# A two-layer graph network on one core: clearing behind the gathers taken out, narrower sums, and 48 tiles fetched row by row by SyncE

## The chip, the cores and the metric

The kernel runs on one core of one Trainium2 chip. The metric is the device time of one execution in microseconds. TensorE (PE) multiplies matrices, VectorE (DVE) and ScalarE (ACT) work on tiles and copy out of the accumulators, GpSimd (POOL) issues the indirect gathers, and SyncE (SP) and ScalarE issue the other transfers.

## The reference

The graph has 12500 nodes with 128 features, 200000 edges sorted by their destination, and 8 relations. Two layers are run, then a residual and a layer norm. Cut to what matters:

```python
W = jnp.einsum('rb,bio->rio', comp, basis)
xw = jnp.einsum('ni,rio->nro', x, W)
msgs = xw[src, et]
seg = dst * N_REL + et
summed = segment_sum(msgs, seg)          # N_NODES * N_REL segments
cnt = segment_sum(ones, seg)
mean = summed / maximum(cnt, 1.0)[:, None]
h_new = relu(mean.reshape(N_NODES, N_REL, HIDDEN).sum(1) + x @ root + bias)
h = h_new + h                            # two layers of this
out = layernorm(x + h)
```

## The kernel before

**Tiles and octets.** The edges are cut into 1563 tiles of 128 in the order of their destinations; eight tiles are an octet (`Q = 8`, 196 octets, numbered `o` in layer 1 and `q` in layer 2). A tile of source rows is fetched by one indirect gather on POOL, a row of 512 bytes for each of the 128 edges.

**Layer 1.** For octet `o`, `gathers` puts the eight gathers of octet `o + 5` on POOL (`AHEAD = 5`, into one of seven `rows` buffers), `means` multiplies the eight row tiles by one-hot matrices that DVE makes, `product` multiplies by the weights, `place` and `finish` add up the nodes. `table` multiplies the finished nodes by layer 2's eight weight matrices and stores the result in DRAM as `y_d`, one row for each node and relation. In the octets from 96 to about 160 DVE, PE and SP also sort the edges of the routed octets (below): SP stores `lo_d` and `sc_d`, two small transfers for each.

**Layer 2** has two ways for an octet. In an ordinary octet POOL gathers rows of `y_d`, eight gathers, and `slot_sums` and `place_sums` add them up. A routed octet (`ROUTED`: octet 7 and every third after it, 62 in all) gets its sums from the node features that already lie on the chip: `compare` makes one-hot matrices on DVE, `pick_rows` picks the rows on PE (L1885), `slots_in` makes matrices of slots on DVE (L1852), `add_up` adds the picked rows into slots (L1905), and `relate` multiplies by the eight relations' weights (L1927). A slot is a node of the octet with a relation. The octet's eight tiles are taken as two parts of four (`BT = 4`), each with `NW = 40` nodes, so that `SEG = 8 * 40 = 320` slots go to each of two accumulators and `relate` gives 80 rows. Edges that found no place are fetched by one gather more (`gather_left`, L778). The steps of a routed octet are spread over the three octets ahead of it. So three octets in a row hold two ordinary ones and a routed one: 17 gathers on POOL, and one routing on PE and DVE.

**The clearing.** Behind each of layer 2's gathers POOL clears 256 bytes in each partition of a tile `blank` that nothing reads (`pause`, L712), and ahead of that it waits for the clearing before.

**Order.** The class `Plan` records every operation in program order with what it reads and writes, and derives the semaphore waits; nothing is reordered. Each engine runs its own operations in that order. Gathers have four semaphores in turn, SP's transfers eight. A gather into a `rows` buffer waits for the PE operation that read it last, so that POOL can run ahead of PE by the buffers it has. For the last six octets (`LATE = 6`) a gather also waits for PE's sums of the octet before (`after`). SP brings the node features (`load_x`), stores the sorted lists, and in layer 2 fetches for each routed octet a list of 256 KB and a small one (`fetch`, `fetch_rows`), when DVE has done with the buffer.

Of the kernel before, what the change touches and what calls it, by code (L numbers as in the profile page):

```python
# [9 lines left out]
F16 = mybir.dt.float16  # L10
I32 = mybir.dt.int32
BF16 = mybir.dt.bfloat16
AF = mybir.ActivationFunctionType
# [416 lines left out]
def ordered_path(  # L430
# [61 lines left out]
    FULL = NQ - 4  # L492
    BT = 4
    CAP = 32
    NW = 40
    BU = P // CAP
# [6 lines left out]
    GU = TU * BU  # L503
    SEG = R * NW
    BR = 2
    EVERY = 3
# [4 lines left out]
    NR = len(ROUTED)  # L511
    SORT = 96
    assert D == P and R * K == P and B == BF + 1 and 1 < TL and LAST < P and BF % 4 == 0 and Q == G and N % 2 == 0
    assert ROUTED[-1] < NQ - 4 and LATER % TURN == 0 and SORT + NR + 8 < NG - 16
# [99 lines left out]
    zero_b = part_of(P, "zero")  # L614
    which_b = [part_of(2 * NW, "which", i) for i in range(2)]
    kept_from = free_at
# [54 lines left out]

    plan = Plan(tc, {"hw": 8, "aq": 4, "gq": 4})
    plan.seen, plan.last = {}, {}
# [31 lines left out]
    rows_g = {}  # L705
    blank = keep([P, P // 2], F32, "blank").bitcast(mybir.dt.uint8)
    paused, pauses = tc.alloc_semaphore("s_pause"), [0]

    def pause():
        if pauses[0]:  # L710
            nc.gpsimd.wait_ge(paused, pauses[0])
        nc.gpsimd.memset(blank[:, :256], 0).then_inc(paused, 1)  # L712
        pauses[0] += 1


    def floats(t, n):
# [4 lines left out]
    fix_rows_c, fix_dm_c = ["jmp"], ["mixer"]  # L721
    y_done = [("y_d", j) for j in range(NT - 2)] + [("y_d", j, k) for j in (NT - 2, NT - 1) for k in (0, 1)]

    def gather(l, q):
# [19 lines left out]
        def some(i0, i1):  # L744
            def emit():
                ins = []
                if fixes:
                    ins.append(nc.gpsimd.indirect_dma_start(
                        out=fix_rows, out_offset=None, in_=y_d,
                        in_offset=bass.IndirectOffsetOnAxis(ap=fix_i[:, 0:1], axis=0)))  # L750
                for i in range(i0, i1):
                    ins.append(nc.gpsimd.indirect_dma_start(  # L752
                        out=t[:, i - q * Q, :], out_offset=None, in_=table_t,
                        in_offset=bass.IndirectOffsetOnAxis(ap=ids[:, i:i + 1], axis=0)))
                    if l == 1:
                        pause()
                return ins

            return emit
# [3 lines left out]
        if q == NQ - 2:  # L763
            for h in range(2):
                plan.add("POOL", some(i0 + h * 4, i0 + h * 4 + 4), reads, [cell + (h,)], lane="gq", n=4, after=after)
        elif l == 1 and q == NQ - 1:
            for i in range(n):
                plan.add("POOL", some(i0 + i, i0 + i + 1), reads, [cell + (i,)], lane="gq", n=1, after=after)
        else:
            plan.add("POOL", some(i0, i0 + n), reads,  # L770
                     [cell + (0,), cell + (1,)] + (fix_rows_c if fixes else []), lane="gq",
                     n=n + fixes, after=after)

    def gather_left(i):
        t, c = left_rows_b[i % len(left_rows_b)]

        def emit():
            ins = nc.gpsimd.indirect_dma_start(out=t, out_offset=None, in_=y_d,  # L778
                                               in_offset=bass.IndirectOffsetOnAxis(ap=idl[:, i:i + 1], axis=0))
            pause()  # L780
            return [ins]

        plan.add("POOL", emit, [idl_b[1]] + y_done, new(c), lane="gq", n=1)
# [402 lines left out]
    def onehot(l, q, g=None):  # L1186
# [11 lines left out]
        if l == 1 and q in ROUTED:  # L1198
            i = ROUTED.index(q)
            o, c = pl[q] = pl2_r.take()  # L1200
            vec(lambda: nc.vector.tensor_scalar(o[:2 * NW], cols[:2 * NW], pos2[:2 * NW, i:i + 1], None,
                                                op0=ALU.is_equal), ["cols", "pos2"], new(c))
# [101 lines left out]
    def means(o, half=None):  # L1304
# [4 lines left out]
        def some(i0, i1):  # L1309
            def emit():  # L1310
                for i in range(i0, i1):
                    last = nc.tensor.matmul(s_b[i // 4][0][:, i % 4, :], t[:, i, :],  # L1312
                                            d[:, i, :], start=True, stop=True)
                return last
# [5 lines left out]
        else:  # L1320
            pe(some(0, n), [c + (0,), c + (1,)] + dc,
               [s_b[h][1] for h in range(-(-n // 4))] + [("done", 0)])
# [170 lines left out]
    def values():  # L1493
# [10 lines left out]
        vec(lambda: nc.vector.memset(zero_at[0:1], 1.0), [], [zero_b[1]])  # L1504
        for b in range(2):
            vec(lambda b=b: nc.vector.memset(which_b[b][0][0:1, b * NW:(b + 1) * NW], 1.0), [], [which_b[b][1]])
        yield
# [28 lines left out]
        yield vec(lambda: nc.vector.tensor_scalar(i2, i1, float(NW), None, op0=ALU.mult), [ta_b[1]], [tb_b[1]])  # L1536
        vec(lambda: nc.vector.tensor_scalar(tb[:, :, BT:], tb[:, :, BT:], float(SEG), None, op0=ALU.add), [], [tb_b[1]])
        n4 = of_routed(near).rearrange("p n (b k) -> p n b k", k=BT)
        f0 = pt[:, 0, :2 * NR].rearrange("p (n b) -> p n b", b=2)
        pe(lambda: nc.tensor.matmul(f0, zero_at, n4[:, :, :, 0], start=True, stop=True), [zero_b[1]] + nears, [pc])  # L1540
        for b in range(2):
            pe(lambda b=b: nc.tensor.matmul(pt[:2 * NW, 1, :NR], which_b[b][0], n4[:, :, b, 0], start=b == 0,
                                            stop=b == 1), [which_b[b][1]] + nears, [pc])
        local = ta.rearrange("p n (b k) -> p n b k", k=BT)
        vec(lambda: nc.vector.tensor_tensor(local, n4, f0.unsqueeze(3).to_broadcast([P, NR, 2, BT]), op=ALU.subtract),
            nears + [pc], [ta_b[1]])
        vec(lambda: nc.vector.tensor_scalar(at_n[:, 1:2], part_f, float(NW), float(-NW), op0=ALU.is_ge, op1=ALU.mult),
            ["part_f"], ["at_n"])
        vec(lambda: nc.vector.tensor_tensor(at_n[:, 0:1], part_f, at_n[:, 1:2], op=ALU.add), ["part_f"], ["at_n"])
        yield vec(lambda: nc.vector.tensor_scalar(pos2[:2 * NW], pt[:2 * NW, 1, :NR], at_n[:2 * NW, 0:1], None,  # L1550
                                                  op0=ALU.add), [pc, "at_n"], ["pos2", "spread"])
        vec(lambda: nc.vector.tensor_tensor(val[:, :, :, 1], ta, tb, op=ALU.add), [ta_b[1], tb_b[1]], [val_b[1]])
# [176 lines left out]
    slot_b += [home(("sT1", "idx", "idx")[i], 2 * SEG, "slot", 5 + i) for i in range(3)]  # L1729
    sum_b = [home(("yr0", "yr1")[i], R * BR * NW, "sum", i) for i in range(2)]  # L1730
    segs_b = home("yr1", SEG, "segs")
# [164 lines left out]
    def add_up(t):  # L1896
# [14 lines left out]
        if u == NU - 1:  # L1911
            t_s, sc = sum_b[i % 2]
            t4 = t_s.rearrange("p (r b n) -> p r b n", r=R, b=BR)
            for k, (b, bc) in enumerate(seg_b):
                copy(t4[:, :, k, :], b.rearrange("p t d -> p (t d)")[:, :SEG].rearrange("p (r n) -> p r n", r=R), [bc],
                     new(sc + (k,)) if (sc + (k,)) in old else [sc + (k,)])
                plan.mark("ACT")

    for i in range(2):
        for k in range(BR):  # L1920
            old[sum_b[i][1] + (k,)] = old[sum_b[i][1]]

    def relate(i):
        t_s, sc = sum_b[i % 2]
        t4 = t_s.rearrange("p (r b n) -> p r b n", r=R, b=BR)
        b, bc = misc
        pe(in_turn([lambda r=r: nc.tensor.matmul(  # L1927
            b[:BR * NW, 0, :], t4[:, r].rearrange("p b n -> p (b n)"), w_sb[:, 1, r, :], start=r == 0, stop=r == R - 1)
            for r in range(R)]), [sc + (k,) for k in range(BR)] + [("w", 1, r) for r in range(R)], [bc])
        plan.mark("PE")  # L1930
        o, c = ys[ROUTED[i]] = ys_r.take()
        copy(o[:BR * NW], b[:BR * NW, 0, :], [bc], [c])
        plan.mark("ACT")
# [52 lines left out]
    def slot_sums(q):  # L1986
# [5 lines left out]
        def emit():  # L1992
            for i in range(Q):
                last = nc.tensor.matmul(m0[i // 2 * 2 * K:(i // 2 + 1) * 2 * K, :], d[:, i, :], t[:, i, :],  # L1994
                                        start=i % 2 == 0, stop=i % 2 == 1)
            return last

        pe(emit, [c + (0,), c + (1,), dc], [bc, ("done", 1)])
        plan.mark("PE")
# [4 lines left out]
    def place_sums(q, k, opens, last):  # L2004
# [4 lines left out]
        reads = [c, oc]  # L2009
        m = 2 * NW if q in ROUTED else P  # L2010
        if root_in:
# [267 lines left out]
    for o in range(NG - 3):  # L2279
# [3 lines left out]
        means(o)  # L2283
        batch(o)
        if o == 1:
            where()
# [134 lines left out]
    for q in range(NQ):  # L2421
# [28 lines left out]
        if q == 0:  # L2450
            turn_last()
        if q == FROM - 1:
            compare(0)
# [105 lines left out]
```

## Time and profile before

| what | value |
|---|---|
| median of 3 runs | 3645.96 us (3643.89 to 3647.16) |
| the profiled execution | 3643.43 us, its span 3641.3 us |
| busy in the span | PE 2870.5 us, POOL 2942.4 us, DVE 2290.1 us, ACT 665.8 us |
| gathers of layer 1 | 1563, mean 957 ns |
| gathers of layer 2 | 1067, mean 953 ns, and 62 of `gather_left` |
| clearings | 1129, mean 329 ns |
| mean granted clock of TensorE | 0.893 of full speed |

In the profile a row of the groups gives the line of the code, the engine, the operation, the tiles written and read, the shape and the count, then the busy time in us and the mean of one in ns, and the time that the engine stood idle ahead of it with what ended most of that wait. "issue" is time in which an engine waited for nothing that the profile shows. Matmuls of 32-bit numbers stand twice in the records: a product of eight matrices reads x16. In the rows by windows each engine's busy time in the stretch is followed by the number of its instructions.

### The profile page before, as it was taken

Reading aid. Unit: us, or ns where it says so; the run is one execution under the profiler, and the core shown is the slowest. Engines: PE = TensorE matmul, PEld = TensorE weight load, DVE = VectorE, ACT = ScalarE, POOL = GpSimd, SP = SyncE. Lnnn points to the kernel's source line nnn. Section 1 sums busy time; section 2 is a strip of 40 time slices with the busy share of each in tenths; the row PEclk is TensorE's granted clock in tenths of the full one; section 3 lists DMA queues with packets and bytes.
Section 4 is the critical chain, followed back from the end, with each engine's and each line's share of the span. In section 5 each row is a group of like instructions: output and inputs, shape, how many; then the busy total and the mean of one; then the engine's idle time right before and its main releaser. Section 6 shows DMA issues by size and latency. Waiting matters only on the chain.

```text
span 3641.3 us, 68810 instructions
## 1 busy us (share of the span) xinstructions
PE 2870.5 (79%) x27639; PEld 2299.7 (63%) x27639; DVE 2290.1 (63%) x6306; ACT 665.8 (18%) x1725; POOL 2942.4 (81%) x3830
## 2 busy tenths in 40 slices
PE   6777667777677777777777499999989988998994
PEld 4665556666666666666665267767666666666663
DVE  5655444543478787873331378877777777786773
ACT  1121112222222222222222011111111111111110
POOL 7777777777777777777776888888888888888887
PEclk8998888888888888888889799999999999999997
DMA  4221233333222222223333322222222222222221
GB/s 132 59 54 53 53 88 99 92 99 99 82 77 82 76 76 77 76 73 99 94 99 106 86 59 59 71 70 65 65 67 71 59 70 67 59 71 67 65 59 55
DMA packets 134922, 275.89 MB, mean 76 GB/s; under 512 B 56995, under 2 KB 65741, under 8 KB 134597
## 3 DMA queue, kind: packets, MB, share of 16 engines
q0 software_dynamic: 86176, 176.66, 18.8%
q1 hardware_dynamic: 31450, 42.72, 3.9%
q10 hardware_dynamic: 16971, 52.05, 3.7%
q8 instruction: 219, 3.59, 0.4%
q14 instruction: 106, 0.87, 0.1%
HBM read 211.95 MB, written 59.28 MB: 74 GB/s over the span
## 4 chain that ended last, share of the span: by engine, by line
POOL 65%; issue 15%; PE 13%; DVE 3%; DMA 2%; ACT 1%; POOLq 0%; ACTq 0%; DVEq 0%
POOL rows L752 55%; POOL blank L712 8%; PE s L1312 2%; PE pt L1885 2%; PE y L1344 2%; PE y L1905 1%; POOL arena L778 1%; PE po L1905 1%; DVE dm L1219 1%; DMA rows<-in_x_dram,idx 1%; PE pt L1443 1%; PE ct L958 1%; DVE arena L948 1%; DMA rows<-y_d,idy 1%; PE s L2025 1%
## 5 line engine op out<-in xcount | busy, mean ns | idle before, releaser
L752 POOL DMA_INDIRECT rows<-in_x_dram,idx x1563 | 1496.0, 957 | 478.1 <-issue 471.1
L752 POOL DMA_INDIRECT rows<-y_d,idy x1067 | 1016.8, 953 | 195.2 <-issue 175.4
L1312 PE MATMUL s<-dm,rows 128*128 128x128 f32 x3126 | 544.8, 347 | 403.1 <-DMA rows<-in_x_dram,idx 383.8
L1312 PEld LDWEIGHTS s<-dm,rows 128*128 128x128 f32 x3126 | 509.0, 255 | 469.2 <-issue 319.1
L1219 DVE TENSOR_SCALAR dm<-cols,kr,w 128x128 f32<-128x128 f16 x1563 | 525.3, 401 | 226.2 <-PE ct L1443 133.9
L1344 PE MATMUL y<-w_sb,sT 128*128 128x128 f32 x3136 | 460.6, 310 | 45.8 <-ACT sT L692 45.6
L1344 PEld LDWEIGHTS y<-w_sb,sT 128*128 128x128 f32 x3136 | 446.4, 227 | 56.2 <-ACT sT L692 54.1
L1885 PE MATMUL pt<-arena,dm 128*32 128x128 f32 x12152 | 408.9, 283 | 5.1 <-DVE dm L1835 4.6
L1885 PEld LDWEIGHTS pt<-arena,dm 128*32 128x32 f32 x12152 | 337.9, 114 | 57.2 <-issue 39.9
L712 POOL MEMSET blank<- 128x256 uint8 x1129 | 371.0, 329 | 0.7
L692 ACT ACTIVATE sT<-s 128x512 f32<-128x512 f32 x391 | 212.2, 594 | 841.7 <-PE s L1312 841.7
L1905 PE MATMUL y<-arena,dm 128*128 128x320 f32 x620 | 242.0, 473 | 35.2 <-DVE arena L1852 34.8
L1178 DVE TENSOR_SCALAR sT<-cols,kr,w 128x32 f32<-128x32 f16 x1040 | 238.3, 302 | 19.3 <-PE s L2029 19.2
L1835 DVE TENSOR_TENSOR dm<-arena,cols 128x768 f32<-128x768 f16 x248 | 231.6, 934 | 5.4 <-DMA arena<-lo_d 3.3
L1905 PE MATMUL po<-arena,dm 128*128 128x320 f32 x620 | 219.1, 435 | 0.0
L1396 DVE TENSOR_TENSOR po<-po,carry 128x128 f32<-128x128 f32 x98 | 28.8, 294 | 299.9 <-PE ct L1443 146.0
L692 ACT ACTIVATE dm<-pt 128x256 f32<-128x256 f32 x248 | 95.0, 383 | 585.3 <-PE pt L1885 585.3
L1994 PE MATMUL ct<-rows,sT 128*32 128x128 f32 x2080 | 91.5, 291 | 115.0 <-DMA rows<-y_d,idy 115.0
L1905 PEld LDWEIGHTS y<-arena,dm 128*128 128x128 f32 x620 | 105.2, 194 | 93.8 <-DVE arena L1852 35.1
L1852 DVE TENSOR_SCALAR arena<-cols,comp_sb 128x640 f32<-128x640 f16 x155 | 140.3, 938 | 37.5 <-DMA arena<-y_d,arena 37.5
L692 ACT ACTIVATE y_row<-pt 128x512 f32<-128x512 f32 (+1 forms) x133 | 79.4, 597 | 413.8 <-PE ct L1443 182.8
L1994 PEld LDWEIGHTS ct<-rows,sT 128*32 128x32 f32 x2080 | 55.3, 113 | 157.1 <-DMA rows<-y_d,idy 75.9
(336 smaller groups left out, 3987.4 us busy)
## 6 DMA issues: line engine op xcount, KB each, us to landing
y_d<-y_row ACTq DMA_DIRECT2D x96, 512.0 KB
rows<-in_x_dram,idx POOLq DMA_INDIRECT x1563
rows<-y_d,idy POOLq DMA_INDIRECT x1067
arena<-lo_d SPq DMA_DIRECT2D x62, 256.0 KB
x_g<-in_x_dram SPq DMA_DIRECT2D x24, 512.0 KB
out_dram<-x_g SPq DMA_DIRECT2D x12, 512.0 KB
arena<-in_L_gnn_basis_dram SPq DMA_DIRECT2D x2, 512.0 KB
w_d<-y_row SPq DMA_DIRECT2D x2, 512.0 KB
```

The lines of the kernel that those rows point to most:

```text
L692: act(lambda: nc.scalar.activation(out_t, in_t, AF.Copy), reads, writes)
L712: nc.gpsimd.memset(blank[:, :256], 0).then_inc(paused, 1)
L752: ins.append(nc.gpsimd.indirect_dma_start(out=t[:, i - q * Q, :], out_offset=None, in_=table_t, in_offset=bass.IndirectOffsetOnAxis(ap=ids ...
L1178: vec(in_turn([lambda i=i: nc.vector.tensor_scalar(t[:, i, :], cols[:, :2 * K], kr[:, i0 + i:i0 + i + 1], w[:, i0 + i:i0 + i + 1], op0=ALU ...
L1219: emits.append(lambda i=i: nc.vector.tensor_scalar(t[:, i - q * Q, :wide], cols[:, :wide], ids[:, i:i + 1], w[:, i:i + 1], op0=ALU.is_equa ...
L1312: last = nc.tensor.matmul(s_b[i // 4][0][:, i % 4, :], t[:, i, :], d[:, i, :], start=True, stop=True)
L1344: last = nc.tensor.matmul(y[:m], t[:, r, :nt, :].rearrange("p t k -> p (t k)"), w_sb[:, 0, r, :], start=(r == 0), stop=(r == R - 1))
L1835: emits = [lambda: nc.vector.tensor_tensor(o[:, :3 * n].rearrange("p (j c) -> p j c", j=3), bits[:, None, u * n:(u + 1) * n].to_broadcast( ...
L1852: vec(lambda v=v, o=o: nc.vector.tensor_scalar(o, segs_p, sg[:, v:v + 1], sg[:, NTL + v:NTL + v + 1], op0=ALU.is_equal, op1=ALU.mult), ["n ...
L1885: last = nc.tensor.matmul(b[k * CAP:(k + 1) * CAP, x, :], o[:n, c:c + CAP], hT[:n, j * P:(j + 1) * P], start=jj == 0, stop=jj == SIZE[g] - 1)
L1905: last = nc.tensor.matmul(b.rearrange("p t d -> p (t d)")[:, :SEG], g[:, x * P:(x + 1) * P], o[:, k * SEG:(k + 1) * SEG], start=v == 0, st ...
L1994: last = nc.tensor.matmul(m0[i // 2 * 2 * K:(i // 2 + 1) * 2 * K, :], d[:, i, :], t[:, i, :], start=i % 2 == 0, stop=i % 2 == 1)
```

## The change

It has four parts. `pause` and its tile are gone. The routed octets' slots are numbered over one span of `NW = 76` nodes for all eight tiles, so that there are 608 slots, 304 to each accumulator, and `relate` gives 76 rows; the preparation in `values` is shorter for it. For 27 tiles of layer 1 (tile 183 and every 50th after it) and 21 of layer 2 (tile 95 and every 72nd) POOL issues no gather: SP issues 128 transfers of one row each into one of two buffers, in 8 chunks of 16, and each chunk first loads 16 addresses from DRAM into SP's registers. The scratch of GpSimd's transfers is 8192 in place of the default.

```diff
-    NW = 40
+    NW = 76
-    SEG = R * NW
-    BR = 2
+    SEG = R * NW // 2
+    RC = 16
+    SINGLES = [("SP", 0, range(183, NQ * Q - 80, 50)), ("SP", 1, range(95, (NQ - 4) * Q, 72))]
...
-    plan = Plan(tc, {"hw": 8, "aq": 4, "gq": 4})
+    plan = Plan(tc, {"hw": 8, "aq": 4, "gq": 4, "sr": 8, "ar": 8})
-    def pause():
-        if pauses[0]:
-            nc.gpsimd.wait_ge(paused, pauses[0])
-        nc.gpsimd.memset(blank[:, :256], 0).then_inc(paused, 1)
-        pauses[0] += 1
+    def single_rows(l, o):
+        for i, (e, at_l, ts) in enumerate(SINGLES):
+            if at_l != l:
+                continue
+            t8 = (x if l == 0 else y_d).bitcast(U8)
+            for k, t in enumerate(ts):
+                for c in range(P // RC):
+                    if (t - ts.step - 2 * Q + c * ts.step * RC // P) // Q != o:
+                        continue
+                    b = hw_b[e][k % 2].bitcast(U8)
+
+                    def emit(e=e, i=i, k=k, c=c, b=b):
+                        eng = by[e]
+                        eng.reg_load(regs[e], off_d[i][k:k + 1, c * RC:(c + 1) * RC])
+                        return [eng.dma_start(b[c * RC + j:c * RC + j + 1, :], bass.AP(
+                            tensor=t8.tensor, offset=eng.snap(r), ap=[[4 * D, 1], [1, 4 * D]]))
+                            for j, r in enumerate(regs[e])]
+
+                    plan.add(e, emit, [("off", i)] + (y_done if l else []), [("hw_" + e, k % 2, c)],
+                             lane="sr" if e == "SP" else "ar", n=RC)
...
                 for i in range(i0, i1):
+                    if (l, i) in SINGLE:
+                        continue
                     ins.append(nc.gpsimd.indirect_dma_start(
...
-                    if l == 1:
-                        pause()
...
-    nc = _bacc.Bacc("TRN2", target_bir_lowering=False, num_devices=1)
+    nc = _bacc.Bacc("TRN2", target_bir_lowering=False, num_devices=1, dynamic_dma_scratch_size=8192)
```

The program's order shows the parts at three places. On POOL, in layer 2, before: the end of one octet, the gather of a routed octet's left edges (`arena<-y_d,arena`) and the start of the next octet.

```order
L752 DMA rows_105<-y_d,idy 128x128
L712 MEMSET blank 128x256 [waits s_pause]
L778 DMA arena<-y_d,arena 128x128 [waits s_gq3,s_DVE]
L712 MEMSET blank 128x256 [waits s_pause]
L752 DMA rows_106<-y_d,idy 128x128 [waits s_PE]
L712 MEMSET blank 128x256 [waits s_pause]
L752 DMA rows_106<-y_d,idy 128x128
```

The same place after, where octet 11 has one of its eight tiles from SP and so only seven gathers.

```order
L800 DMA rows_105<-y_d,idy 128x128 [waits s_gq2,s_PE]
L800 DMA rows_105<-y_d,idy 128x128 x7
L824 DMA arena<-y_d,arena 128x128 [waits s_gq3,s_DVE]
L800 DMA rows_106<-y_d,idy 128x128 [waits s_PE]
L800 DMA rows_106<-y_d,idy 128x128 x6
```

Nothing stands between two gathers any more, and the waits for PE and DVE are at the places where they were.

On SP, in the sorting part of layer 1, before: the two stores of three octets.

```order
L689 DMA lo_d<-arena 32x32 [waits s_ACT]
L689 DMA sc_d<-arena 32x2x32 [waits s_ACT]
L689 DMA lo_d<-arena 32x32 [waits s_ACT]
L689 DMA sc_d<-arena 32x2x32 [waits s_ACT]
L689 DMA lo_d<-arena 32x32 [waits s_ACT]
L689 DMA sc_d<-arena 32x2x32 [waits s_hw3,s_ACT]
```

After, chunks of rows (`TENSOR_LOAD` is the load of 16 addresses, `x16` the 16 transfers) stand between the stores; the next rows of the order go on in the same way.

```order
L699 DMA lo_d<-arena 32x32 [waits s_ACT]
L699 DMA sc_d<-arena 32x2x32 [waits s_ACT]
L752 TENSOR_LOAD off_d_156 [waits s_sr0]
L753 DMA hw_SP_152<-in_x_dram 1x512 x16
L752 TENSOR_LOAD off_d_156 [waits s_sr1]
L753 DMA hw_SP_152<-in_x_dram 1x512 x16
L699 DMA lo_d<-arena 32x32 [waits s_ACT]
L699 DMA sc_d<-arena 32x2x32 [waits s_ACT]
```

A store now has up to 32 transfers ahead of it on SP, and the chunks wait in turn behind the stores, which wait for ACT. In layer 2 the fetches stand between the chunks in the same way.

On PE, in layer 2, after: the routed octet's sums and the octet whose eighth tile (`hw_SP_152`) SP has brought.

```order
L1941 MATMUL y<-arena,dm 128x304
L1941 MATMUL po_138<-arena,dm 128x304
L2029 MATMUL ct<-rows_106,sT_112 32x128 [waits s_sr4,s_sr3,s_sr5,s_sr2,s_sr6,s_sr1,s_sr7,s_sr0,s_gq0]
L2029 MATMUL ct<-rows_106,sT_112 32x128 x6
L2029 MATMUL ct<-hw_SP_152,sT_112 32x128
L2062 MATMUL s_135<-pl_116,ys_118 128x256
```

Before, the same place reads:

```order
L1905 MATMUL y<-arena,dm 128x320
L1905 MATMUL po_138<-arena,dm 128x320
L1994 MATMUL ct<-rows_106,sT_112 32x128 [waits s_gq0]
L1994 MATMUL ct<-rows_106,sT_112 32x128 x7
L2025 MATMUL s_135<-pl_116,ys_118 128x256
```

The order of PE's work is the same; the sums are 304 wide in place of 320, and the whole octet waits for the eight chunks of its row-by-row tile.

More of the change, by code (lines that the diff above doesn't have):

```diff
@@ L11 @@
 I32 = mybir.dt.int32
+U8 = mybir.dt.uint8
 BF16 = mybir.dt.bfloat16
@@ L512, in ordered_path @@
     SORT = 96
+    RC = 16
+    SINGLES = [("SP", 0, range(183, NQ * Q - 80, 50)), ("SP", 1, range(95, (NQ - 4) * Q, 72))]
+    SINGLE = {(l, t): (i, k) for i, (_, l, ts) in enumerate(SINGLES) for k, t in enumerate(ts)}
+    LISTED = (14, NQ - 24)
+    assert all(l == 0 or all(t // Q not in ROUTED and t // Q < NQ - 4 for t in ts) for _, l, ts in SINGLES)
+    assert len(SINGLE) == sum(len(ts) for _, _, ts in SINGLES)
     assert D == P and R * K == P and B == BF + 1 and 1 < TL and LAST < P and BF % 4 == 0 and Q == G and N % 2 == 0
@@ L670, in ordered_path @@
     nb_f = keep([1, 1], F32, "nb_f")
-    plan = Plan(tc, {"hw": 8, "aq": 4, "gq": 4})
+    hw_b = {e: [keep([P, D], F32, f"hw_{e}{i}") for i in range(2)] for e in {e: 0 for e, _, _ in SINGLES}}
+    offs = [keep([P, len(ts)], I32, f"off{i}") for i, (_, _, ts) in enumerate(SINGLES)]
+    off_d = [dram.tile([len(ts), P], I32, name=f"off_d{i}") for i, (_, _, ts) in enumerate(SINGLES)]
+    by = {"SP": nc.sync, "ACT": nc.scalar}
+    regs = {e: [by[e].alloc_register(f"row_{e}{i}") for i in range(RC)] for e in hw_b}
+    plan = Plan(tc, {"hw": 8, "aq": 4, "gq": 4, "sr": 8, "ar": 8})
     plan.seen, plan.last = {}, {}
@@ L722, in ordered_path, with single_lists, single, singles_in @@
     y_done = [("y_d", j) for j in range(NT - 2)] + [("y_d", j, k) for j in (NT - 2, NT - 1) for k in (0, 1)]
+    def single_lists(l):
+        for i, (_, at_l, ts) in enumerate(SINGLES):
+            if at_l != l:
+                continue
+            ids, name = (idx, "idx") if l == 0 else (idy, "idy")
+            n = len(ts)
+            blocks_i = range(ts.start // P, ts[-1] // P + 1)
+            picked = ids[:, ts.start:ts.start + n * ts.step].rearrange("p (n k) -> p n k", k=ts.step)[:, :, 0]
+            vec(lambda i=i, picked=picked: nc.vector.tensor_single_scalar(
+                offs[i], picked, 9, op=ALU.logical_shift_left),
+                [(name, b) for b in blocks_i], [("offs", i)])
+            plan.mark("DVE")
+            load(bass.AP(tensor=off_d[i].tensor, offset=off_d[i].offset, ap=[[1, P], [P, n], [1, 1]]),
+                 offs[i].unsqueeze(2), [("offs", i)], [("off", i)])
+    def single_rows(l, o):
+        for i, (e, at_l, ts) in enumerate(SINGLES):
+            if at_l != l:
+                continue
[13 more added lines that the diff above has]
+                             lane="sr" if e == "SP" else "ar", n=RC)
+    def single(l, t):
+        if (l, t) not in SINGLE:
+            return None
+        i, k = SINGLE[l, t]
+        e = SINGLES[i][0]
+        return hw_b[e][k % 2], [("hw_" + e, k % 2, c) for c in range(P // RC)]
+    def singles_in(l, i0, i1):
+        return [single(l, i) for i in range(i0, i1) if (l, i) in SINGLE]
     def gather(l, q):
@@ L1729, in ordered_path @@
     slot_b += [home(("sT1", "idx", "idx")[i], 2 * SEG, "slot", 5 + i) for i in range(3)]
[L1730 removed]
+    sum_b = [home(("yr0", "yr1")[i], 2 * SEG, "sum", i) for i in range(2)]
     segs_b = home("yr1", SEG, "segs")
@@ L1919, in ordered_path @@
     for i in range(2):
-        for k in range(BR):
+        for k in range(len(seg_b)):
             old[sum_b[i][1] + (k,)] = old[sum_b[i][1]]
```

60 lines of the change are left out of this document (26 added, 34 removed).

## The prediction

> **What bounds the kernel now.** I read the busy time in slices and the chain of waits first (the page), then POOL's groups, then single stages in the windows.
>
> ```profile
> PE   6777667777677777777777499999989988998994
> ...
> POOL 7777777777777777777776888888888888888887
> PEclk8998888888888888888889799999999999999997
> ...
> POOL 65%; issue 15%; PE 13%; DVE 3%; DMA 2%; ACT 1%; POOLq 0%; ACTq 0%; DVEq 0%
> POOL rows L752 55%; POOL blank L712 8%; PE s L1312 2%; PE pt L1885 2%; PE y L1344 2%; PE y L1905 1%; POOL arena L778 1%; PE po L1905 1%; DVE dm L1219 1%; DMA rows<-in_x_dram,idx 1%; PE pt L1443 1%; PE ct L958 1%; DVE arena L948 1%; DMA rows<-y_d,idy 1%; PE s L2025 1%
> ```
>
> 80% of the chain is POOL and the gaps between its instructions; 8% are the clearings. But PE is at 9 tenths in layer 2 (the last 17 slices), so PE stands close behind POOL there. POOL's groups and their pace by stage (the windows of L752, then of L712, columns: stretch, length, busy and count):
>
> ```profile
> L752 POOL DMA_INDIRECT rows<-in_x_dram,idx x1563 | 1496.0, 957 | 478.1 <-issue 471.1
> L752 POOL DMA_INDIRECT rows<-y_d,idy x1067 | 1016.8, 953 | 195.2 <-issue 175.4
> L712 POOL MEMSET blank<- 128x256 uint8 x1129 | 371.0, 329 | 0.7
> ```
>
> ```profile
> 30.00:690.00 660.00, 499.11 (x529) 0.87 0.25 71
> 1000.00:1600.00 600.00, 457.37 (x469) 0.83 0.27 77
> ...
> 2094.00:3540.00 1446.00, 328.98 (x1001) 0.97 0.25 66
> ```
>
> In layer 1 a gather takes 660/529 = 1.248 us from start to start (0.96 of work, 0.30 of gap), in the sorting stage 600/469 = 1.279. In layer 2 one comes every 1446/1001 = 1.445 us: 0.95 of gather, 0.165 of gap, 0.33 of clearing. "issue" ends 471 of the 478 us of idle time in the one layer and 175 of 195 in the other, so no gather waits long but at the end of layer 1, and both layers go at POOL's pace. How far PE is behind in layer 2 shows in the routed octets, one for every three octets (17 gathers). These rows are the first and the last `relate`, then all engines in two stretches, and the records of `relate` (16 a time) in the first of them:
>
> ```profile
> 2108.84 1.91 PE L1927 MATMUL po<-w_sb,y_row 128*80 128x128 f32 x16
> ...
> 3570.03 3.17 PE L1927 MATMUL po<-w_sb,y_row 128*80 128x128 f32 x14
> ```
>
> ```profile
> 2224.00:2419.00 195.00, 191.65 (x2615) 143.77 (x2614) 164.12 (x421) 33.25 (x98) 172.42 (x271) 1.00 0.26 71
> 2420.00:3540.00 1120.00, 1010.02 (x13267) 755.88 (x13268) 826.85 (x2080) 160.50 (x488) 990.91 (x1551) 0.96 0.25 65
> ```
>
> ```profile
> 2224.00:2419.00 195.00, 17.19 (x144) 16.45 (x145) 1.00 0.26 71
> ```
>
> Over the layer the 61 steps from one routed octet to the next take (3570.03 - 2108.84)/61 = 23.95 us. From 2224 to 2419 us PE is busy 98% at full clock, catching up after a late start: there it does 144/16 = 9 routed octets in 195 us, 21.67 us each. That is PE's own pace, and DVE is at 84% in it. So POOL can become faster by 2.3 us in 24 before PE takes over.
>
> **The clearing.** Its removal shortens a gather's period in layer 2 from 1.445 to about 1.248 us if the gap behind a gather is then 0.30 as in layer 1. Layer 2 has one gather with nothing behind it:
>
> ```profile
> 2019.89 1.22 POOL L748 DMA_INDIRECT jmp<-y_d,fix_i  x1 [1.11 <-DMA y_d<-y_row]
> 2021.42 0.94 POOL L752 DMA_INDIRECT rows<-y_d,idy  x1 [0.30 <-issue]
> ```
>
> The gap is 0.30 there. Below, the bound is 1.248, above it the sorting stage's 1.279, where DVE is at 80%. Three octets cost POOL 17 x 1.248 = 21.2 us, and with 21 gathers fewer over 65 triples 16.67 x 1.248 = 20.8 (21.3 at 1.279).
>
> **The narrower sums.** PE's products with 320 columns follow each other at 0.54 us at full clock:
>
> ```profile
> 2107.76 0.70 PE L1905 MATMUL y<-arena,dm 128*128 128x320 f32 x2
> 2108.30 0.70 PE L1905 MATMUL po<-arena,dm 128*128 128x320 f32 x2
> ```
>
> 304 columns make 0.513. A routed octet has 16 of them (eight tiles, two accumulators): 0.43 us less, 21.67 - 0.43 = 21.24. DVE's slots shrink in the same share, off the path. If the octets' spans were over 76 nodes, the kernel would take its general path; in the inputs the widest of the 62 has 69.
>
> So PE (21.24) and POOL (20.8 to 21.3) come out nearly equal, and PE is a little behind. I take 21.3 a step, PE's pace and little for the waits that two equal engines cause. The bounds: 20.8, if PE's 2% of idle time in that stretch also goes, and 21.67/0.96 = 22.6, if the narrower sums give nothing and the clock stays at the second stretch's 0.96. The forecast is 61 x (23.95 - 21.3) = 162 us, with ends of 192 and 82.
>
> **The start and the end of layer 2.** DVE and so PE wait for the first gather of left edges:
>
> ```profile
> DVE arena L1852 <- DMA arena<-y_d,arena: 37.5, 1, 37.5
> ...
> L778 POOL DMA_INDIRECT arena<-y_d,arena x62: 950/950/953, 2079.1 to 3577.0; - x62
> ```
>
> It has 56 ordinary gathers of layer 2 ahead of it on POOL (octets 0 to 6): 56 x 0.197 = 11 us earlier. At the end the gathers of the last octets wait for PE's sums, so that POOL's pace counts again: octets 191 to 194 and the three tiles of octet 195 are 35 gathers, 35 x 0.197 = 7 us.
>
> **The rows by SP.** In layer 1 they take 27 gathers off POOL, 10 of them in the sorting stage: 17 x 1.248 + 10 x 1.279 = 34 us, if SP keeps up. In layer 2 the 21 are already in the 20.8. The price of a row on SP isn't in the trace. The nearest issue is that of a single run, the others are SP's loads of one word and its register work:
>
> ```profile
> L689 SPq DMA_DIRECT2D arena<-in_edge_type_dram x1: 249/249/249, 11.6 to 11.6; - x1
> ...
> L689 SPq DMA_DIRECT2D sc_d<-arena x62: 368/423/762, 998.0 to 1624.9; - x62
> ```
>
> ```profile
> L2184 SPq TENSOR_LOAD <-bad x1: 498/498/498, 2828.1 to 2828.1; - x1
> L2184 SPq FUSED_REGOPS  x1: 192/192/192, 2828.7 to 2828.7; - x1
> L2184 SPq SEQ_ASSERT  x1: 28/28/28, 2828.9 to 2828.9; - x1
> ```
>
> ```profile
> 4.02 0.37 ACTq L689
> 4.40 0.04 issue
> ```
>
> A row is one register move and one issue. With 0.25 for the issue, 0.03 to 0.19 for the move and a gap of 0.04 behind each (the last fence, from the chain of the first 25 us, where ACT issues transfers one behind the other), it costs 0.36 to 0.52 us; I take 0.37, nearest to the small instruction, since a move is one step and not several fused. A chunk's load costs at least 0.50 + 0.04, so a tile costs SP 128 x 0.37 + 8 x 0.54 = 52 us (71 at 0.52). Layer 1 gives it 50 x 1.248 = 62 us and layer 2 nine octets, 3 x 21.3 = 64. In the sorting stage SP also issues two stores, 0.30 and 0.42 us, in each octet of 10.2 us: 1.28 chunks of 6.5 and 0.8 make 9.1 of 10.2. So SP is hidden behind POOL at 0.37, is filled in the sorting stage from 0.42 and everywhere from 0.45. Behind SP's rows stand `lo_d`, `sc_d` and layer 2's fetches, each delayed by a chunk or two (7 to 13 us); the buffers that they free or fill are wanted two octets (16 us) later or more. On PE the octet with such a tile waits for its eight chunks, and behind that wait stands the next routing; SP has the last chunk issued some 22 tiles (27 us) ahead. I cost both at nothing; when this lead is gone, the first rival begins.
>
> [...]
>
> **The scratch.** [...] A gather lands 2.5 us after its issue, so that two or three are under way:
>
> ```profile
> 283.90 2.48 DMA rows<-in_x_dram,idx
> ```
>
> [...]
>
> **The sum.** 34 + 11 + 162 + 7 = 214 us off the profiled execution's 3643.4: 3429. The median of the runs is 2.5 us above that execution, so 3432.
>
> **The rivals.** *SP becomes the bound* (slower). Layer 1's first chunk can go at octet 14, about 155 us; then come 27 tiles, about 80 us of rest of the layer and 20 of its end, 21 tiles, and 60 us to the end: 315 + 48 tiles' price. At 64 us a tile that begins to show; at 69.3, a row of 0.51 us, it is as slow as now, and at the upper bound's 71.4 it gives 3742. The 192 ns speak for it, the 249 and the 28 against. [...]
>
> *The clearing isn't what held the gathers* (the change doesn't do what it says): POOL stays at 1.445 in layer 2, be it by the scratch or by something that the clearing hides. Then only the fewer gathers count, 34 + 21 x 1.445 = 64 us: 3579, with the median's 2.5 some 3582. The gap of 0.30 behind L748 speaks against it.
>
> *PE loses more than it should*: it waits for late rows or left edges in every step and falls to half clock in between (granted 0.96 in the second stretch, 1.00 in the first). At the bound of 22.6 us a step, 61 x 1.3 = 79 us more: 3511.
>
> **How the numbers follow.** Forecast, between 3400 and 3470: 0.67. PE's longer steps, or SP somewhat over its period, 3470 to 3620: 0.19, half of it under 3510. The clearing without effect: 0.05. SP so slow that the kernel is slower than now: 0.07, the 0.02 in it. Below 3400: 0.02. The range is 3398 to 3515; it leaves out some 0.2 above. About 0.2% is what a measurement of this kernel can tell from no change. Faster 0.91, same 0.02, slower 0.07: only SP's row price between 0.505 and 0.51 us would give the same.
>
> **What would show it.** In the changed profile L752's successor has no clearing behind it and 1.25 us from start to start where PE lets it; POOL has waits for PE in layer 2, PE is at 97% or more there at a clock near 1.00, and `relate` comes every 21.3 us. Layer 1 ends 34 us earlier. SP's row issues stand at 0.37 us. Wrong would be: PE waiting for `hw_SP` in both layers (the first rival), gathers still 1.4 us apart with nothing between them (the second), or steps over 22 us with PE idle (the third).

## The result, and the profile after

The changed kernel takes 3798.57 us (median of 4 runs, 3793.73 to 3799.97) against 3644.93 us before (4 runs, 3643.50 to 3647.16), measured side by side: ratio 1.0419, 95% interval 1.0401 to 1.0437. It is slower by 4%; the forecast was 3432 us. The profiled execution took 3793.73 us with a span of 3791.9 us, at a granted clock of 0.862 (before 0.893).

From the page of the changed kernel: busy tenths in the slices of PE and POOL, the granted clock, and the chain of work that ended last, by engine and by line.

```profile
PE   6757455574555666566455558999899899899996
...
POOL 7777777577567566566666457777766766666653
PEclk8988788787787788788778789999999999999998
...
SPq 65%; issue 17%; PE 9%; DVE 3%; DMA 2%; POOL 1%; ACT 1%; ACTq 0%; POOLq 0%; DVEq 0%
SPq L753 39%; SPq L752 19%; SPq L754 5%; SPq L699 2%; PE y L1390 2%; POOL rows L800 1%; PE s L1358 1%; PE pt L1921 1%; DVE dm L1264 1%; PE y L1941 1%; PE pt L1489 1%; PE po L1941 1%; DVE arena L993 1%; DMA off_d<-off 0%; PE ct L1003 0%
```

Before, 80% of this chain were POOL and the gaps between its instructions. Now 65% are SP, and the lines are those of the single rows: the row transfers (L753), the loads of addresses (L752) and a register move (L754). POOL has fallen from 7 and 8 tenths to 5 to 7. SP's work is not in the busy table, since issuing a transfer does not count as busy there; the chain shows it nonetheless.

A stretch of the chain in the middle of layer 1 (start, length, line), with the end of one chunk of 16 rows, a whole chunk, and two loads:

```profile
591.36 0.23 SPq L753
591.74 0.23 SPq L753
592.13 0.23 SPq L753
592.52 0.23 SPq L753
592.75 0.05 issue
592.80 2.04 SPq L752
594.98 0.26 SPq L753
...
600.83 0.23 SPq L753
601.11 1.96 SPq L752
```

A row follows the row before it after 0.39 us, and between two chunks stands a load of some 2 us. SP's instructions over the whole program, grouped by line and tile (min/median/max in ns, first and last start), the fix-up gather that ends layer 1, and `relate`:

```profile
L752 SPq TENSOR_LOAD <-off_d x384: 1878/2004/6879, 195.4 to 3744.7; - x192
...
L753 SPq DMA_DIRECT2D hw_SP<-in_x_dram x3456: 13/228/733, 197.5 to 2115.4; - x192
...
L753 SPq DMA_DIRECT2D hw_SP<-y_d x2688: 227/228/299, 2244.4 to 3753.2; - x192
...
L754 SPq MOVE  x6144: 16/34/312, 197.4 to 3753.0; - x199
```

```profile
L794 POOL DMA_INDIRECT jmp<-y_d,fix_i x1: 1028/1028/1028, 2231.2 to 2231.2; - x1
```

```profile
L1961 PE MATMUL po<-w_sb,y_row x992: 272/273/273, 2312.3 to 3729.4; 128*76 128x128 f32 x199
```

In layer 1 a tile takes SP (2115.4 - 197.5)/27 = 71.0 us, in layer 2 (3753.2 - 2244.4)/21 = 71.8. Layer 1 was to give it 62.4 us a tile and layer 2 some 64. So layer 1 ends late: its fix-up gather starts at 2231.2 us in place of 2019.9, 211 us later. Layer 2 is shorter than before, but its routed octets come every (3729.4 - 2312.3)/61 = 23.2 us, not every 21.3.

Who waits, in the changed kernel (engine, line, what it waited for: us in total, times, longest):

```profile
PE s L1358 <- DMA hw_SP<-in_x_dram: 495.2, 26, 37.6
...
PE po L1899 <- DMA dm<-sc_d: 97.9, 26, 6.8
...
PE ct L2029 <- DMA hw_SP<-y_d: 23.1, 1, 23.1
```

```profile
POOL rows L800 <- PE s L1358: 252.1, 36, 42.3
...
ACT arena L702 <- DMA lo_d<-arena: 239.2, 53, 13.4
...
POOL rows L800 <- PE ct L2029: 183.6, 33, 52.7
...
DVE dm L1871 <- DMA arena<-lo_d: 153.3, 37, 7.5
```

In layer 1 PE waits 26 times for a row tile, once for each tile but one, and POOL then waits for PE to free the buffers. In the sorting stage ACT waits 239 us for SP's stores of `lo_d`, which stand behind rows too. In layer 2 PE hardly waits for the rows themselves (23 us). It waits for `sc_d`, and DVE for `lo_d`: the fetches that stand behind the rows on SP. All engines in most of layer 2:

```profile
2260.00:3660.00 1400.00, 1260.98 (x17080) 961.73 (x17081) 1050.41 (x2666) 206.97 (x627) 967.04 (x1025) 0.95 0.26 69
```

In this stretch (length, then busy time and count of PE, PEld, DVE, ACT and POOL, then the clock, DMA share and GB/s) PE is busy 90% at a clock of 0.95; without rows it comes to 98% at 1.00 (the next section).

Eight of the runs below were made while the kernel before itself took 4569 to 4666 us; nothing is concluded from their times, and for that reason all eight kernels were run again.

### The profile page after: what moved, and what is told of

Same layout as the page of the kernel before. It is cut to its first block, busy times and chain, and to the rows that moved or that the text cites. A ratio compares the mean times of both kernels' runs of the same rounds, so it can differ in the third digit from the quotient of the medians.

```text
span 3791.9 us, 86653 instructions
## 1 busy us (share of the span) xinstructions
PE 2711.9 (72%) x27635; PEld 2180.3 (57%) x27635; DVE 2273.5 (60%) x6303; ACT 659.7 (17%) x1725; POOL 2520.9 (66%) x2653
## 4 chain that ended last, share of the span: by engine, by line
SPq 65%; issue 17%; PE 9%; DVE 3%; DMA 2%; POOL 1%; ACT 1%; ACTq 0%; POOLq 0%; DVEq 0%
SPq L753 39%; SPq L752 19%; SPq L754 5%; SPq L699 2%; PE y L1390 2%; POOL rows L800 1%; PE s L1358 1%; PE pt L1921 1%; DVE dm L1264 1%; PE y L1941 1%; PE pt L1489 1%; PE po L1941 1%; DVE arena L993 1%; DMA off_d<-off 0%; PE ct L1003 0%
## 5 line engine op out<-in xcount | busy, mean ns | idle before, releaser
L800 POOL DMA_INDIRECT rows<-in_x_dram,idx x1536 | 1472.9, 959 | 711.7 <-issue 452.8
L800 POOL DMA_INDIRECT rows<-y_d,idy x1046 | 987.4, 944 | 511.2 <-issue 305.8
L1358 PE MATMUL s<-dm,rows 128*128 128x128 f32 x3072 | 423.8, 294 | 523.8 <-DMA hw_SP<-in_x_dram 495.2
L1358 PEld LDWEIGHTS s<-dm,rows 128*128 128x128 f32 x3072 | 402.9, 208 | 564.7 <-issue 534.8
L1941 PE MATMUL y<-arena,dm 128*128 128x304 f32 x620 | 237.2, 465 | 28.6 <-DVE arena L1888 28.6
L1941 PE MATMUL po<-arena,dm 128*128 128x304 f32 x620 | 213.6, 427 | 0.0
L1660 DVE TENSOR_TENSOR arena<-ct,arena 128x256 f32<-128x256 f32 x62 | 26.1, 421 | 216.8 <-PE y L1700 175.0
L1888 DVE TENSOR_SCALAR arena<-cols,comp_sb 128x608 f32<-128x608 f16 x155 | 135.3, 907 | 30.3 <-DMA arena<-y_d,arena 30.3
L1489 PE MATMUL pt<-w_sb,arena 128*128 128x512 f32 (+1 forms) x262 | 141.5, 623 | 9.6 <-ACT y_row L702 8.2
L1941 PEld LDWEIGHTS po<-arena,dm 128*128 128x128 f32 x620 | 121.3, 196 | 43.7 <-issue 4.4
```

Of the source, the lines that this page charges most:

```text
L800: ins.append(nc.gpsimd.indirect_dma_start(out=t[:, i - q * Q, :], out_offset=None, in_=table_t, in_offset=bass.IndirectOffsetOnAxis(ap=ids ...
L1941: last = nc.tensor.matmul(b.rearrange("p t d -> p (t d)")[:, :SEG], g[:, x * P:(x + 1) * P], o[:, k * SEG:(k + 1) * SEG], start=v == 0, st ...
```

## The experiments

Each version was measured side by side with the kernel before on the same chip. The versions were on several chips; on each the kernel before took 3643 to 3645 us. The eight runs set aside stand at the end of this section.

**Without the rows.**

```diff
-    SINGLES = [("SP", 0, range(183, NQ * Q - 80, 50)), ("SP", 1, range(95, (NQ - 4) * Q, 72))]
+    SINGLES = []
```

> [...] Theory A, SP's work on the rows is the whole loss: 3466 us (ratio to before 0.951). Theory B, one of the other three parts cost the time: 3640 us or above (ratio 1.00 or more).

Measured: 3449.48 us (3447.77 to 3452.07), ratio 0.9464 (0.9449 to 0.9480). Its chain, the window from 2094 to 3380 us (columns as above), POOL's gaps without another wait (us in total, times, longest), the end of layer 1 and `relate`:

```profile
PE 45%; POOL 37%; issue 12%; DVE 2%; DMA 2%; ACT 2%; POOLq 0%; ACTq 0%; DVEq 0%
```

```profile
2094.00:3380.00 1286.00, 1262.43 (x17553) 966.00 (x17547) 1070.91 (x2725) 212.76 (x647) 963.98 (x1021) 1.00 0.29 75
```

```profile
POOL rows L800 <- issue: 786.6, 2581, 0.3
```

```profile
L794 POOL DMA_INDIRECT jmp<-y_d,fix_i x1: 1063/1063/1063, 2021.1 to 2021.1; - x1
```

```profile
L1961 PE MATMUL po<-w_sb,y_row x992: 272/273/273, 2102.4 to 3394.4; 128*76 128x128 f32 x199
```

Theory A holds, theory B falls: the rows are the whole loss, and more. Layer 1 ends where it did before. The gap between gathers is 786.6/2581 = 0.30 us. In layer 2 PE is busy 1262/1286 = 98% at full clock, POOL 75%, and a routed octet comes every (3394.4 - 2102.4)/61 = 21.18 us. (The steps here are counted to the last product of the last `relate`; to its first product, as the prediction counts, each is some 0.03 us less.)

**Rows in layer 1 only** (the second entry of `SINGLES` taken out).

> [...] In the changed kernel's trace layer 1 ends 210 us later than without rows (the fix-up gather after it starts at 2231.2 us in place of 2021.1). Theory A (each layer loses by its own tiles, for the same SP): 3449 + 210 = 3660 us, layer 2 at 21.15 us a routed step as without rows; the other 138 us of 3798 are the rows of layer 2. Rival (layer 2's steps of 23.2 us have another cause, such as the late end of layer 1): layer 2 stays near 23.2 us a step, 3780 us.

Measured: 3648.17 us (3645.29 to 3655.82), ratio 1.0008 (0.9999 to 1.0018).

```profile
L794 POOL DMA_INDIRECT jmp<-y_d,fix_i x1: 942/942/942, 2222.4 to 2222.4; - x1
```

```profile
L1961 PE MATMUL po<-w_sb,y_row x992: 272/273/273, 2302.2 to 3594.3; 128*76 128x128 f32 x199
```

Layer 1 loses its 200 us and layer 2 goes at 21.18 us a step, as theory A has it; the rival falls. So of the 349 us that the rows cost against the version without them, 199 are layer 1's (3648.2 - 3449.5) and 150 layer 2's (3798.6 - 3648.2).

**Addresses from SBUF.** A tile's 128 addresses are moved from DRAM into one partition of SBUF by one transfer, two tiles ahead.

```diff
+                    if c == 0 and k + 2 < len(ts):
+                        load(off_s[i][(k + 2) % 3], off_d[i][k + 2:k + 3, :], [("off", i)], [("off_s", i, (k + 2) % 3)])
...
-                        eng.reg_load(regs[e], off_d[i][k:k + 1, c * RC:(c + 1) * RC])
+                        eng.reg_load(regs[e], off_s[i][k % 3][:, c * RC:(c + 1) * RC])
```

> The changed kernel with the addresses loaded from SBUF, 16 at a time. In the trace of the disturbed run a load from SBUF took 1.16 us (median) against 2.00 from DRAM, so a tile costs SP 128 x 0.387 + 8 x 1.2 + 0.4 = 59.5 us, under the 62.4 of layer 1 and the 64 of layer 2, but over 0.9 of both. Theory A2 (the load is what was mis-sized, and the rows run in time once a tile is under its period): 3440 to 3500 us, ratio 0.945 to 0.96. Rival A'' (SP has other work and its chunks hold up what is behind them, so that a filling of 95% is as bad as an overfilled queue): 3600 us or more.

Measured: 3543.49 us (3538.80 to 3550.00), ratio 0.9730 (0.9714 to 0.9746). SP's loads and rows, the fix-up gather and `relate`:

```profile
L758 SPq TENSOR_LOAD <-off_s x384: 973/1221/2499, 196.6 to 3492.0; - x192
...
L759 SPq DMA_DIRECT2D hw_SP<-in_x_dram x3456: 227/228/632, 197.9 to 1981.2; - x192
...
L759 SPq DMA_DIRECT2D hw_SP<-y_d x2688: 227/228/298, 2106.8 to 3499.2; - x192
```

```profile
L800 POOL DMA_INDIRECT jmp<-y_d,fix_i x1: 1013/1013/1013, 2094.9 to 2094.9; - x1
```

```profile
L1967 PE MATMUL po<-w_sb,y_row x992: 272/273/273, 2175.9 to 3483.8; 128*76 128x128 f32 x199
```

The time lies between the two forecasts, because the tile takes (1981.2 - 197.9)/27 = 66.0 us, not 59.5. The rows come to 0.405 us each on the mean (0.387 is what they take undisturbed), and SP has other transfers and waits of 4 us a tile. Layer 1 is still over-filled (66.0 against 62.4), layer 2 a little (66.3 against 63.5). Layer 1 ends 74 us later than without rows, and a step of layer 2 is (3483.8 - 2175.9)/61 = 21.44 us. So the rival's case, a filling of 95%, didn't arise here. The cheaper load, with one small transfer a tile added for it, moved the time by 255 us.

**Loads of 32 addresses.**

```diff
-    RC = 16
+    RC = 32
```

> The changed kernel with 32 addresses in a load in place of 16, run again for the same reason; the disturbed run's loads had a median of 3.74 us. Theory A2 (a load costs by the word, 0.11 us each, with 0.26 us beside them): a tile's eight or four loads cost 16.1 or 15.0 us, so a tile is 1.2 us shorter, 71 us become about 70, and 48 x 1.2 = 58 us go: 3740 us. Theory A1 (2.0 us a load however many words): 8 us a tile go, SP comes under its period in layer 2 and near it in layer 1: 3550 or less.

Measured: 3728.66 us (3723.48 to 3732.81), ratio 1.0226 (1.0209 to 1.0243).

```profile
L752 SPq TENSOR_LOAD <-off_d x192: 3524/3798/13904, 197.8 to 3675.8; - x192
```

Twice the words took 3.80 us in place of 2.00. A load from DRAM so cost some (3.80 - 2.00)/16 = 0.112 us a word with some 0.2 us beside them, an estimate that takes the cost to run in a line through these two counts; theory A1 falls.

**A longer period.** Loads from DRAM as in the changed kernel, rows for fewer tiles: one tile in 64 of layer 1 (21 tiles, 64 x 1.248 = 80 us for each) and one in 96 of layer 2 (15 tiles, 4 x 21.15 = 85 us for each).

```diff
-    SINGLES = [("SP", 0, range(183, NQ * Q - 80, 50)), ("SP", 1, range(95, (NQ - 4) * Q, 72))]
+    SINGLES = [("SP", 0, range(199, NQ * Q - 80, 64)), ("SP", 1, range(119, (NQ - 4) * Q, 96))]
```

> [...] SP took 71 to 72 us a tile in the changed kernel. Theory A (only over-filling hurts): both fit, 3449 - 21 x 1.25 = 3423 us, layer 2 at 21.15 us a step. Rival (rows hurt the fetches of the routing that stand behind them on SP even when SP has room): layer 1 gains its 26 us, layer 2 stays over 21.6 us a step, 3450 us or more.

Measured: 3427.56 us (3424.37 to 3430.54), ratio 0.9410 (0.9394 to 0.9426).

```profile
L752 SPq TENSOR_LOAD <-off_d x288: 1872/2012/4362, 195.0 to 3294.1; - x144
```

```profile
L794 POOL DMA_INDIRECT jmp<-y_d,fix_i x1: 943/943/943, 1997.0 to 1997.0; - x1
```

```profile
L1961 PE MATMUL po<-w_sb,y_row x992: 272/273/273, 2077.6 to 3369.7; 128*76 128x128 f32 x199
```

The loads are as dear as in the changed kernel, and the step is 21.18 us. So the fetches behind the rows don't suffer as long as SP has this much room (71 us in 80, 72 in 85): the rival falls, and over-filling is what hurt. Where between this filling of 0.89 and the 1.04 of layer 2 with addresses from SBUF it begins to hurt was not tried. Layer 2's 15 tiles change nothing, since PE sets the pace there; layer 1's 21 bring the 22 us: it ends 24 us earlier than without rows.

**Rows in layer 1 alone, with room and loads from SBUF.**

```diff
-    SINGLES = [("SP", 0, range(183, NQ * Q - 80, 50)), ("SP", 1, range(95, (NQ - 4) * Q, 72))]
+    SINGLES = [("SP", 0, range(215, NQ * Q - 80, 60))]
...
```

The rest of the edit is that of the addresses from SBUF.

> Rows in layer 1 alone, for one tile in 60 from tile 215 on (22 tiles), addresses loaded from SBUF; the rest as changed; run again for the same reason. SP measured 66 us a tile with all else that it does in layer 1, and gets 60 x 1.248 = 75 us. Theory A (rows pay where POOL is the bound and SP has room): 22 x 1.25 = 27 us under the version without rows, 3422 us. Rival (the octet with such a tile costs PE more than a gather saves): 3449 or more.

Measured: 3424.61 us (3422.37 to 3425.93), ratio 0.9392 (0.9376 to 0.9407). It is the fastest version here, 6.1% under the kernel before. The fix-up gather stands at 1998.2 us, 22.9 earlier than without rows:

```profile
L800 POOL DMA_INDIRECT jmp<-y_d,fix_i x1: 1105/1105/1105, 1998.2 to 1998.2; - x1
```

**The clearing alone.** The kernel before, without its two calls of `pause`.

```diff
-                    if l == 1:
-                        pause()
...
-            pause()
```

> The kernel before without the clearing behind layer 2's gathers, and nothing else changed: sums of two times 40 nodes with 320 columns, the whole scratch, no rows; run again for the same reason. Theory (POOL held layer 2, then PE does at 21.67 us a step): 61 x (21.67 - 21.15) = 32 us over the 3449 of the version without rows, 3480 us. Rival 1 (the sums over 76 nodes and half the scratch save nothing): 3449. Rival 2 (the clearing was not what held the gathers): 3640.

Measured: 3479.05 us (3477.23 to 3481.56), ratio 0.9550 (0.9534 to 0.9566).

```profile
L1924 PE MATMUL po<-w_sb,y_row x992: 272/273/273, 2101.8 to 3419.8; 128*80 128x128 f32 x199
```

A step is (3419.8 - 2101.8)/61 = 21.61 us. The clearing is worth 3643.5 - 3479.1 = 164 us. The sums over 76 nodes then take 21.61 - 21.18 = 0.43 us off a step, 26 of the 29.6 us between 3479.1 and 3449.5. Both rivals fall.

**The whole scratch**, in the version without rows (`dynamic_dma_scratch_size=8192` taken out).

> The changed kernel without the rows, as in the run of 3449 us, and with the whole of the DMA scratch again; run again for the same reason. Theory (half of it holds enough gathers): 3449, ratio 0.946. Rival (the half holds some gathers back): 3440 or less, with more gathers under way at a time.

Measured: 3450.66 us (3450.03 to 3453.62), ratio 0.9471 (0.9455 to 0.9486), the same as 3449.48 with half of it.

**The runs set aside.** The same kernels as above, on two other chips; from none of the times is anything concluded. On the first the kernel before took 4666.01 us. Without rows, 4902.80 us:

> The changed kernel without any single-row transfer: all gathers on POOL, the rest of the change (no clearing, sums over 76 nodes, half the scratch) kept. Theory A, SP's work on the rows is the whole loss: layer 1 goes as before (1.248 us a gather), layer 2 at 21.3 us a routed step, so 3432 + 34 = 3466 us. Theory B, one of the other three parts cost the time: the clearing was needed or half the scratch holds the gathers back, layer 2 stays at 1.445 us a gather or more, 3640 us or above.

Loads of 32 addresses, 5761.45 us:

> The changed kernel with 32 addresses in a load in place of 16, so 4 loads a tile in place of 8. A row takes 0.387 us from start to start, a tile's 128 rows 49.5 us. If a load costs 2.0 us as a whole, however many words it brings (theory A1), a tile takes 49.5 + 4 x 2.05 = 57.7 us, under the 62 us that layer 1 gives it, and the time falls to some 3450 us. If it costs by the word, (2.0 - 0.5)/15 = 0.10 us each beside the one-word load's 0.50 (theory A2), a load of 32 takes 3.7 us, a tile 64.5 in place of 66, and 48 x 1.6 = 77 us go: some 3720 us. Theory B (SP isn't the cause): 3798.

Addresses from SBUF, 5675.55 us:

> The changed kernel with the addresses of a tile first moved from DRAM to SBUF, one small transfer a tile, and loaded into the registers from there, 16 at a time as before. The one-word load of 0.50 us, from which the prediction took the price, reads SBUF; the loads of 2.0 us read DRAM. If the memory makes the difference (theory A3), a load takes about 0.5 us, a tile 49.5 + 8 x 0.55 + 0.4 = 54 us, and the time falls to some 3440 us. If the count of words does (theory A2), the load stays near 2.0 us and the time near 3800, 10 us more at most for the added transfers.

The longer period, 5349.02 us:

> The changed kernel with rows brought for one tile in 64 of layer 1 (21 tiles, every 80 us at 1.248 us a gather) and one in 96 of layer 2 (15 tiles, every 85 us at 21.3 us a routed step), in place of one in 50 and one in 72. SP needs some 66 us a tile, 71 with what else it does. Theory A, SP was over-filled: it now fits, PE no longer waits for the rows, 3466 - 21 x 1.25 = 3440 us, layer 2 at 21.3 us a routed step. Rival A', the rows hurt what is queued behind them on SP even when SP fits, since each fetch of a routing waits for a chunk of 8 us: layer 2 stays over 22.5 us a step, 3515 us or more.

On the second the kernel before took 4568.69 us. Rows in layer 1 only, 5445.94 us:

> The changed kernel with its 27 tiles of rows in layer 1 and none in layer 2. In the changed kernel's trace layer 1 ends 210 us later than without rows (the fix-up gather after it starts at 2231.2 us in place of 2021.1). Theory A (each layer loses by its own tiles, for the same SP): 3449 + 210 = 3660 us, layer 2 at 21.15 us a routed step as without rows; the other 138 us of 3798 are the rows of layer 2. Rival (layer 2's steps of 23.2 us have another cause, such as the late and uneven end of layer 1): layer 2 stays near 23.2 us a step, 3780 us.

The clearing alone, 4846.04 us:

> The kernel before without the clearing behind layer 2's gathers, and nothing else changed: sums of two times 40 nodes with 320 columns, the whole scratch, no rows. Theory (POOL held layer 2, then PE does at 21.67 us a step): 61 x (21.67 - 21.15) = 32 us over the 3449 of the version without rows, 3480 us. Rival 1 (the sums over 76 nodes saved nothing): 3449. Rival 2 (the clearing was not what held the gathers): 3640.

The whole scratch, 4824.59 us:

> The changed kernel without the rows, as in the run of 3449 us, and with the whole of the DMA scratch again. Theory (half of it holds enough gathers): 3449, ratio 0.946. Rival (the half holds some gathers back): 3435 or less, with shorter gaps between gathers than 0.30 us.

Rows in layer 1 with room and loads from SBUF, 5087.17 us:

> Rows in layer 1 alone, for one tile in 60 from tile 215 on (22 tiles), addresses loaded from SBUF; the rest as changed. SP measured 66 us a tile with all else that it does in layer 1, and gets 60 x 1.248 = 75 us. Theory A (rows pay where POOL is the bound and SP has room): 22 x 1.25 = 27 us under the version without rows, 3422 us. Rival (the octet with such a tile costs PE more than a gather saves): 3449 or more.

## Why the prediction was wrong, step by step

- **The failed step is the price of a chunk's load on SP.** The prediction wrote that it "costs at least 0.50 + 0.04", from a load of one word out of SBUF, and put that lower end into the sum, with no upper end. A load of 16 words out of DRAM took 2.00 us, four times as long. Eight of them a tile are 16 us in place of 4. With 0.54 us a load and all else as measured below, a tile would be some 51.9 + 4.3 + 2.4 = 58.6 us, under both layers' periods; that is an estimate, no run has it. The runs show a cost that grows with the count: 112 ns a word from DRAM (3.80 us for 32 against 2.00 for 16) and, by 1.22 us for 16 words against 0.50 for one, 48 ns from SBUF, each an estimate worked out from two counts only.
- **The row's price was nearly right.** Forecast 0.37 us, measured 0.387 in an undisturbed chunk: 0.228 for the issue, and two register moves (0.034 and 0.029) where one was counted. On the mean a row takes 0.405.
- **SP's other work was counted only in the sorting stage.** Summed over SP's records from 197.5 to 2115.4 us, a tile takes 51.9 us for rows and their moves, 16.8 for loads and 2.4 for other transfers. Each class has the gaps behind its records in it. That makes the 71, against the 52 in the forecast. The excess over the period nearly accounts for layer 1: 27 x (71.0 - 62.4) = 232 us, against 211 us of lateness and some 28 that 27 tiles would have brought, at 22.9 us for 22.
- **The first rival came about, with a larger fixed part.** Its formula had 315 us beside the 48 tiles; the trace has 195 us until the first load, 129 between the layers' rows and 39 at the end, 363. With 48 x 71.4 us that is 3790, the span but for 2 us. Its chance was put at 0.07 because only the row's bounds (0.36 to 0.52) went into it; the load's price had no spread at all. No run shows a ground for the 0.02 within it: a row took 0.387 us undisturbed and 0.405 on the mean. At 2.0 us a load the forecast's own row of 0.37 gives 128 x 0.37 + 8 x 2.04 = 63.7 us, which already fills layer 1 and all but fills layer 2. That the rival's upper price of a tile, 71.4 us, is the measured mean is chance: it stood for rows of 0.52 us, and 128 x 0.52 + 8 x 0.54 is 70.9, with which the rival's formula gives 3718 us and not 3742.
- **The rows in front of the routing's fetches were costed at nothing, on the condition of a lead.** With room on SP that held (21.18 us a step with the sparser tiles). Without it PE waited 98 us for `sc_d`, its clock was 0.95 and not 1.00, and layer 2's step rose to 23.2 us. That is beyond the third rival's bound of 22.6 and has its form, late lists and a lower clock; it came with SP's over-filling and was gone without rows, where PE stands at 98% and a clock of 1.00.
- **The clearing, right.** The gap of 0.30 us was as forecast, and POOL gave way to PE in layer 2. The second rival had no part.
- **The sums, right.** 0.43 us a step forecast, 21.61 - 21.18 = 0.43 measured; 21.3 us a step forecast, 21.18 measured without rows.
- **The scratch** has no term in the sum, and none was missing: without rows 3450.66 us with the whole of it, 3449.48 with half.
- **The rows' gain where POOL is the bound, nearly right:** 1.25 us a gather forecast; 22 tiles brought 24.9 us and 21 tiles 21.9, some 1.1 each. In layer 2, where PE is the bound, they bring nothing, as the step of 21.18 us with and without them shows.
- **Start and end of layer 2:** 11 and 7 us forecast. Without rows the first `relate` stands 6.4 us earlier than before (2102.4 against 2108.84) and the time behind the last is some 13 us shorter (3641.3 - 3573.2 before, 3450.3 - 3394.7 without rows), nearly the same in sum, though neither term was met.

Without rows the other terms of the prediction give 3466 us, and 3449.48 was measured. That its 3432 us stands 7 us from the version in which 22 tiles of rows fit is in part luck: the rows were to bring 34 us and brought 25, and the rest brought more than forecast.

## What to carry to other kernels

When an idle engine takes over work, add up everything it issues per period, with an upper as well as a lower price for each instruction, and let it have room: at 66 us of 62 the rows lost all and more, at 66 of 75 they brought nearly their full gain. A price that a trace shows for one word from one memory is no price for sixteen from another (0.50 us against 2.00 here); "at least" is a bound for the range and not a term of the sum. Look first at which engine is the bound in each stage, since rows taken off POOL pay only in the stage that POOL holds.

## What the hardware showed that was not expected

A register load by SP took 0.50 us for one word from SBUF (the kernel before, L2184), 1.22 us for 16 from SBUF (L758 with addresses from SBUF), 2.00 us for 16 (the changed kernel, L752) and 3.80 us for 32 from DRAM (L752 with loads of 32). A single-row transfer with its address in a register took two moves (0.034 and 0.029 us) ahead of the issue of 0.228 us, and followed the one before after 0.387 us.

In the runs set aside the version without rows had this chain:

```profile
PE 45%; another core or an unknown queue 36%; issue 11%; ACT 6%; DVE 2%; DMA 0%; ACTq 0%; DVEq 0%
```

There the five versions with rows lost more against the kernel before (1.1145 to 1.2348) than the three without, and even the version without rows lost to it (1.0516 and not 0.9464). In the eight chains 8 to 36% are waits for "another core or an unknown queue", of which the other runs' chains show none. What those waits were for no trace shows, and the cause stays open. The gains above are shown only where the kernel before takes some 3644 us.
